# Layer 0's experts: slot comparisons and return matrices written entry by entry, behind the gathered rows

## The chip, the core and the metric

The kernel runs on one core of one Trainium2 chip. The metric is the device time of one execution in microseconds (us), as the median of several runs. The core has a matrix engine (PE, with its weight loads shown apart as PEld), a vector engine (DVE), an activation engine (ACT), a general engine (POOL) and a queue engine for transfers (SP). Each engine works through its own list of instructions in order; an instruction whose input is late holds back all that stand behind it on that engine.

## The reference

The whole program is a decoder of two layers over x of 8 entries, 256 tokens and 256 features: self attention, cross attention and a feed-forward part, twice. The change lies in the feed-forward part of layer 0. There each of 8 experts chooses the 32 tokens (256 / 8) for which it has the largest gates, works on their normed rows, scales the results by the gate values and writes them back to their tokens. The write is a "set": where several experts chose one token, the last of them counts.

```python
def _L0_ffn_ref(x, gate_w, experts):
    B, N, D = x.shape
    E = gate_w.shape[-1]
    M = N // E
    gate_logits = jnp.einsum('bnd,de->bne', x, gate_w)
    competitive_gates = sinkhorn(gate_logits)
    vals, idx = jax.lax.top_k(jnp.swapaxes(competitive_gates, -1, -2), M)
    gate_values = jnp.swapaxes(vals, -1, -2)
    routed_indices = jnp.swapaxes(idx, -1, -2)
    b_idx = jnp.arange(B)[:, None, None]
    routed = x[b_idx, routed_indices]
    routed = jnp.transpose(routed, (2, 0, 1, 3))
    outputs = jnp.einsum('ebmd,edf->ebmf', routed, experts)
    outputs = outputs * jnp.transpose(gate_values, (2, 0, 1))[..., None]
    vals_bmed = jnp.transpose(outputs, (1, 2, 0, 3))
    routed_back = jnp.zeros_like(x).at[b_idx, routed_indices].set(vals_bmed)
    return routed_back

x = x + _L0_ffn_ref(_layernorm(x, axis=-1), L0_ffn_gate_w, L0_ffn_experts)
```

## The kernel before

All of x stays on the chip. The attention parts are a list of 24 units: for each pair of entries two self attentions and two cross attentions of layer 0, then eight self attentions of layer 1. A loop goes through the units. The core of a unit has eight pieces: score products `st` (L334), exponentials `pT` (L343), value products `o` (L366), and after the second group of heads a copy of `o` to `oT` on DVE (L387). Behind each piece the loop emits a piece of the neighbouring units (the end of the one before, the preparation of the one after), and then one step of the experts, `next(experts_at)`. The experts are written as a generator, `chosen_experts(b0, nb)`, that works on a group of two entries (nb = 2) and pauses at each `yield`. There are four groups. So the sequence of the program interleaves three streams.

The order of the program is not yet the order on the engines. A planner in the build step places each instruction by its position in the program, as a rank, and by when it takes its inputs to be there; it may set a later instruction ahead of an earlier one on the same engine. The order that came out can be read in the trace.

The preparation of a self attention unit runs, for each of two halves of the tokens, the products `qk` and `v` (L274), the rotation `qc` and `qs` on DVE (L413, L429), in layer 0 an addition to `qc` on POOL (L464), and the sum `qkr` (L465), on POOL for the first half and on DVE for the second. Then PE transposes `qkr` twice: `tr` (L283), which is copied to `kT`, and `qps` (L474), which becomes `qm` (L312, L310).

In a group of the experts:

- the gates are formed and balanced, and the 32 best tokens of each of 8 experts and 2 entries are found on DVE (L671 to L675). That gives 256 slots per entry. Their token numbers and gate values go to memory and come back in two layouts: `idx_row` (the 256 token numbers of an entry along the free side, in all partitions) and `by_half`;
- six steps pass, then PE turns `by_half` into `cps` (L689) and DVE copies it to `col` (L691): for each half of the slots of an entry, the token number and gate value of each slot, one per partition;
- **slot comparisons** (L696): for each entry and half one operation on DVE compares the token numbers of all slots (`idx_row`) with that of the slot in the partition (`col`), multiplies by `later` (1 where the other slot comes later) and sums into a column of `over`. A slot with `over` zero is the last for its token. Two small operations (L706, L707) make `weight` from this: the gate value where `over` is zero, else 0. They work on the four columns of the group at once;
- per entry: two **gathering matrices** `pick` (L714) and two **matrices of the return** `put` (L715), 128x256 each, made on POOL by comparing with a constant row; a `yield`; PE forms the gathered rows `rps` (L274), ACT copies them to `rT` (L722); a `yield`; PE multiplies by the experts, `y` (L728), DVE scales by `weight` into `ys` (L738); a `yield`; PE multiplies by `put`, `back` (L274), and DVE adds that to x (L745).

In the program a group's step with `col` and the comparisons comes after `values(0)` and the first half's `qk` of a unit; the first entry's `pick` and `put` after the next scores; its `rps` after `values(1)`, the copy to `oT` and the second half's `qk` and rotation. The second entry's steps follow behind the first entry's `back`; its `rps` falls in the next unit. Each small tile (`put`, `pick`, `junk`, `weight` and others) has two buffers.

Of the kernel before, what the change touches and what calls it, by code (L numbers as in the profile page):

```python
# [28 lines left out]
F32 = mybir.dt.float32  # L29
# [4 lines left out]
ALU = mybir.AluOpType  # L34
# [4 lines left out]
P = 128  # L39
B, S, D = 8, 256, 256  # L40
# [115 lines left out]
def plain(  # L156
# [4 lines left out]
    nc = tc.nc  # L161
# [83 lines left out]
    def norm_stats(views, eps, pool, tag):  # L245

        n = len(views)
        st = pool.tile([P, 2, 6], F32, tag=f"{tag}st", name=f"{tag}st")
        mv = pool.tile([P, 2, 2], F32, tag=f"{tag}mv", name=f"{tag}mv")
        for i, v in enumerate(views):  # L250
            nc.vector.bn_stats(st[:, i, :], v)
            nc.vector.bn_aggr(mv[:, i, :], st[:, i, :])
        ve = pool.tile([P, 2], F32, tag=f"{tag}ve", name=f"{tag}ve")
        nc.vector.tensor_scalar(ve[:, :n], mv[:, :n, 1], eps, None, ALU.add)  # L254
        rs = pool.tile([P, 2], F32, tag=f"{tag}rs", name=f"{tag}rs")
        nc.gpsimd.tensor_tensor(rs[:, :n], ve[:, :n], mhalf[:, :n], ALU.pow)  # L256
        return mv, rs

    def normed(dst, src, mv, rs, i):
        return nc.vector.tensor_scalar(dst, src, mv[:, i, 0:1], rs[:, i : i + 1], ALU.subtract, ALU.mult)  # L260
# [332 lines left out]
    bwork = w_exp.enter_context(tc.tile_pool(name="b2", bufs=2, side="right"))  # L593
    experts = one.tile([P, E, 2, D], F32, name="experts")
    later = one.tile([P, 2, S], F32, name="later")
    num = one.tile([P, S], F32, name="num")
# [32 lines left out]
    def chosen_experts(b0, nb):  # L629

        xn = bwork.tile([P, 2 * nb, D], F32, tag="xnb", name="xnb")
        g = bwork.tile([P, nb, 2, E], F32, tag="g", name="g")
        for b in range(nb):
            mv, rs = norm_stats([x[:, 2 * (b0 + b) + t, :] for t in range(2)], 1e-5, small, "ln")
            for t in range(2):
                normed(xn[:, 2 * b + t, :], x[:, 2 * (b0 + b) + t, :], mv, rs, t)
            xnT = transposed(xn[:, 2 * b : 2 * b + 2, :], work, mm, "xnT")
            yield
            lg = mm.tile([P, 2, D], F32, tag="mm", name="lg")
            for t in range(2):  # L640
                for c in range(2):
                    product(lg[:, t, :E], xnT[:, c, bass.ts(t, P)], gate[:, c, :], c == 0, c == 1)
            nc.vector.tensor_scalar(g[:, b], lg[:, :, :E], 1e-6, None, ALU.max)
            yield

        gt = bwork.tile([P, 2, nb, E], F32, tag="gt", name="gt")
        for it in range(8):
            cs = mm.tile([P, nb, E], F32, tag="mm", name="cs")
            for t in range(2):
                product(cs, ones, g[:, :, t, :], t == 0, t == 1)  # L650
            rc = bwork.tile([P, nb, E], F32, tag="rc", name="rc")
            nc.vector.reciprocal(rc, cs)
            nc.vector.tensor_tensor(g, g, rc.unsqueeze(2).to_broadcast([P, nb, 2, E]), ALU.mult)
            rsum = bwork.tile([P, nb, 2], F32, tag="rsum", name="rsum")
            nc.vector.tensor_reduce(rsum, g, AX.X, ALU.add)
            rr = bwork.tile([P, nb, 2], F32, tag="rr", name="rr")
            nc.vector.reciprocal(rr, rsum)
            dst = gt.rearrange("p t b e -> p b t e") if it == 7 else g
            nc.vector.tensor_tensor(dst, g, rr.unsqueeze(3).to_broadcast([P, nb, 2, E]), ALU.mult)
            yield  # L660


        vps = mm.tile([nb * E, S], F32, tag="mm", name="vps")
        for t in range(2):
            nc.tensor.transpose(vps[:, bass.ts(t, P)], gt[:, t].rearrange("p b e -> p (b e)"), ident)
        v = bwork.tile([nb * E, S], F32, tag="v", name="v")
        nc.scalar.copy(v, vps)
        top = bwork.tile([nb * E, 2, TOP], F32, tag="top", name="top")
        place = bwork.tile([nb * E, TOP], U32, tag="place", name="place")
        for r in range(0, TOP, 8):  # L670
            nc.vector.max(top[:, 1, r : r + 8], v)  # L671
            nc.vector.max_index(place[:, r : r + 8], top[:, 1, r : r + 8], v)
            if r + 8 < TOP:
                nc.vector.match_replace(v, top[:, 1, r : r + 8], v, NEG)
        nc.vector.tensor_copy(top[:, 0, :], place)  # L675

        slots = dram.tile([2, nb * S], F32, name=f"slots{b0}")
        nc.sync.dma_start(slots.rearrange("k (q r) -> q k r", r=TOP), top)
        idx_row = bwork.tile([P, nb, S], F32, tag="idx_row", name="idx_row")
        nc.sync.dma_start(  # L680
            idx_row.rearrange("p b s -> p (b s)"), slots[0:1, :].to_broadcast([P, nb * S])
        )
        by_half = bwork.tile([2 * nb, 2, P], F32, tag="by_half", name="by_half")
        nc.sync.dma_start(by_half, slots.rearrange("k (q s) -> q k s", s=P))
        for _ in range(6):
            yield
        cps = mm.tile([P, 2, 2 * nb], F32, tag="mm", name="cps")
        for k in range(2):
            nc.tensor.transpose(cps[:, k, :], by_half[:, k, :], ident[: 2 * nb, : 2 * nb])  # L689
        col = bwork.tile([P, 2, 2 * nb], F32, tag="col", name="col")  # L690
        nc.vector.tensor_copy(col, cps)  # L691
        over = bwork.tile([P, 2 * nb], F32, tag="over", name="over")
        for q in range(2 * nb):
            b, h = q // 2, q % 2
            junk = bwork.tile([P, S], F32, tag="junk", name="junk")
            nc.vector.scalar_tensor_tensor(  # L696
                junk,
                idx_row[:, b, :],
                col[:, 0, q : q + 1],
                later[:, h, :],  # L700
                ALU.is_equal,
                ALU.mult,
                accum_out=over[:, q : q + 1],
            )
        weight = bwork.tile([P, 2 * nb], F32, tag="weight", name="weight")
        nc.vector.tensor_scalar(weight, over, 0.0, None, ALU.is_equal)  # L706
        nc.vector.tensor_tensor(weight, weight, col[:, 1, :], ALU.mult)  # L707
        yield

        for b in range(nb):  # L710
            pick = bwork.tile([P, 2, S], F32, tag="pick", name="pick")
            put = bwork.tile([P, 2, S], F32, tag="put", name="put")
            for t in range(2):
                nc.gpsimd.tensor_scalar(pick[:, t, :], idx_row[:, b, :], tokid[:, t : t + 1], None, ALU.is_equal)  # L714
                nc.gpsimd.tensor_scalar(put[:, t, :], num, col[:, 0, 2 * b + t : 2 * b + t + 1], None, ALU.is_equal)  # L715
            yield
            rps = mm.tile([P, 2, S], F32, tag="mm", name="rps")
            for c in range(2):
                for t in range(2):
                    product(rps[:, c, :], xn[:, 2 * b + t, bass.ts(c, P)], pick[:, t, :], t == 0, t == 1)  # L720
            rT = bwork.tile([P, 2, S], F32, tag="rT", name="rT")
            nc.scalar.copy(rT, rps)  # L722
            yield
            y = mm.tile([P, 2, D], F32, tag="mm", name="y")
            for e in range(E):
                rows = slice(TOP * (e % 4), TOP * (e % 4) + TOP)
                for c in range(2):
                    nc.tensor.matmul(  # L728
                        y[rows, e // 4, :],
                        rT[:, c, TOP * e : TOP * (e + 1)],  # L730
                        experts[:, e, c, :],
                        start=c == 0,
                        stop=c == 1,
                    )
            ys = bwork.tile([P, 2, D], F32, tag="ys", name="ys")
            for h in range(2):
                q = 2 * b + h
                nc.vector.tensor_scalar(ys[:, h, :], y[:, h, :], weight[:, q : q + 1], None, ALU.mult)  # L738
            yield
            back = mm.tile([P, 2, D], F32, tag="mm", name="back")  # L740
            for t in range(2):
                for h in range(2):
                    product(back[:, t, :], put[:, h, bass.ts(t, P)], ys[:, h, :], h == 0, h == 1)
            xb = x[:, 2 * (b0 + b) : 2 * (b0 + b) + 2, :]
            nc.vector.tensor_tensor(xb, xb, back, ALU.add)  # L745
            yield
# [2019 lines left out]
```

## Time and profile before

| what | value |
|---|---|
| runs | 1375.85, 1377.11, 1380.27 us; median 1377.11 |
| profiled execution, its own time | 1368.84 us |
| span of its profile | 1367.0 us |
| mean granted clock of PE | 0.993 |
| slot comparisons L696 | 16, median 0.684 us (0.473 to 1.521) |
| weights L706 and L707 | 4 each, median 0.245 and 0.275 us |
| return matrices L715 | 16, median 0.972 us (0.914 to 1.212) |
| gathering matrices L714 | 16, median 0.921 us |
| the four groups, first comparison at | 194.02, 301.14, 405.88, 506.34 us |

Times in the profile are counted from the start of the span. A line of the time order gives the start, the time busy (over several instructions where it ends in x2 or more), engine, line, operation, what is written and read, and in brackets how long the engine had been idle and what ended that. A window's line gives the busy time of each engine in a stretch, with the number of instructions, and behind them the granted clock of PE (1.00 is full), the share of the transfer engines and GB/s.

### The profile page before, as it was taken

How to read it: one execution, taken by the hardware profiler on the slowest of the kernel's cores; microseconds unless marked ns; L12 is line 12 of the kernel's file. 1: busy time of each engine (PE TensorE's matmuls, PEld its weight loads, DVE VectorE, ACT ScalarE, POOL GpSimd, SP SyncE). 2: the span in 40 equal slices, each digit the busy share in tenths (PEclk: the TensorE clock that was granted, in tenths of full speed). 3: DMA queues.
4: the chain of work that ended last, by engine and by line, in shares of the span. 5: the costliest groups of instructions: out<-in, count | busy, mean ns of one | idle time of the engine just before them, and what ended most of it. 6: DMA issues, size and time to landing. Idle time of an engine off the chain costs nothing.

```text
span 1367.0 us, 30959 instructions
## 1 busy us (share of the span) xinstructions
PE 1328.8 (97%) x13210; PEld 924.9 (68%) x13210; DVE 575.7 (42%) x1632; ACT 482.6 (35%) x778; POOL 384.7 (28%) x481
## 2 busy tenths in 40 slices
PE   6999999999999999999999999999999999999998
PEld 3666756755766766665667676776767657688886
DVE  5343463473465564444224323232432447322234
ACT  2455443543543433531313223231322313022222
POOL 4232051051033242420214243241424421400004
PEclk9999999999999999999999999999999999999999
DMA  8970000000000003200011010101101110779954
GB/s 309 337 234 17 9 25 1 17 19 7 2 9 2 2 9 105 106 1 1 17 48 32 17 33 17 34 16 48 33 17 33 65 32 8 285 314 409 394 224 130
DMA packets 46930, 116.71 MB, mean 85 GB/s; under 512 B 8272, under 2 KB 30400, under 8 KB 42432
## 3 DMA queue, kind: packets, MB, share of 16 engines
q1 hardware_dynamic: 38912, 92.74, 19.9%
q0 software_dynamic: 5152, 18.89, 3.8%
q10 hardware_dynamic: 2720, 3.02, 0.6%
q8 instruction: 106, 1.74, 0.5%
q14 instruction: 40, 0.33, 0.1%
HBM read 104.00 MB, written 27.93 MB: 97 GB/s over the span
## 4 chain that ended last, share of the span: by engine, by line
PE 81%; DVE 5%; POOL 5%; issue 3%; ACT 1%; DMA 1%; SPq 0%; POOLq 0%; ACTq 0%; DVEq 0%
PE st L334 9%; PE o L366 9%; PE h L274 6%; PE v L274 6%; PE k L274 5%; PE wo L274 4%; PE ox L1372 4%; PE stx L1334 4%; PE out L1754 3%; PE out L1563 3%; PE qk L274 3%; PE tr L283 3%; PE q L274 2%; PE den L1348 2%; PE ao L274 2%
## 5 line engine op out<-in xcount | busy, mean ns | idle before, releaser
L366 PE MATMUL o<-pT,padv 128*64 128x256 f32 (+1 forms) x1536 | 172.6, 367 | 0.9 <-POOL pT L346 0.9
L343 ACT ACTIVATE pT<-st 128x1024 f32<-128x1024 f32 (+1 forms) x128 | 110.6, 915 | 87.6 <-PE st L334 86.4
L366 PEld LDWEIGHTS o<-pT,padv 128*64 128x64 f32 x1536 | 103.6, 138 | 53.7 <-issue 11.6
L334 PE MATMUL st<-qm,kT 64*128 64x256 f32 (+1 forms) x1024 | 116.9, 366 | 0.7 <-DVE qm L312 0.6
L334 PEld LDWEIGHTS st<-qm,kT 64*128 64x128 f32 x1024 | 89.6, 188 | 26.1 <-issue 15.8
L1340 POOL TENSOR_TENSOR both<-pTx 128x512 f32<-128x512 f32 x64 | 82.0, 1305 | 46.0 <-ACT pTx L1338 38.9
L274 PE MATMUL h<-xrT,w 128*64 128x128 f32 (+1 forms) x1936 | 87.0, 250 | 1.1 <-issue 1.1
L274 PEld LDWEIGHTS h<-xrT,w 128*64 128x64 f32 x1936 | 84.4, 137 | 4.0 <-issue 1.7
L343 ACT ACTIVATE pT<-st,kbias 128x1024 f32<-128x1024 f32 x64 | 67.9, 1112 | 28.8 <-PE st L334 28.7
L1338 ACT ACTIVATE pTx<-stx 128x1024 f32<-128x1024 f32 x64 | 62.2, 1022 | 42.3 <-PE stx L1334 40.3
L256 POOL TENSOR_TENSOR lnrs<-lnve,mhalf 128x2 f32<-128x2 f32 x48 | 33.7, 705 | 147.1 <-DVE lnve L254 95.2
L949 DVE TENSOR_TENSOR midr<-sl,h 128x128 f32<-128x128 f32 x102 | 29.3, 288 | 95.3 <-PE h L274 65.3
L334 PE MATMUL st<-qm,memk 64*128 64x256 f32 x512 | 68.8, 393 | 0.4
L1334 PE MATMUL stx<-qTx,kTx 64*128 64x256 f32 x512 | 64.3, 391 | 2.5 <-ACT pTx L1338 2.5
L274 PE MATMUL qk<-l_wqkv,xnT 128*64 128x512 f32 x256 | 62.6, 610 | 0.7 <-ACT xnT L286 0.7
L346 POOL TENSOR_SCALAR_AFFINE_SELECT pT<-pT 128x512 f32<-128x512 f32 x64 | 40.0, 645 | 82.0 <-ACT pT L343 78.7
L1372 PE MATMUL ox<-pTx,vx 128*64 128x256 f32 x512 | 61.1, 381 | 0.0
L948 ACT ACTIVATE sl<-h 128x128 f32<-128x128 f32 (+1 forms) x108 | 31.8, 294 | 79.7 <-PE h L274 55.8
L1334 PEld LDWEIGHTS stx<-qTx,kTx 64*128 64x128 f32 x512 | 46.1, 186 | 20.3 <-ACT pTx L1338 7.2
L274 PE MATMUL wo<-wout_x,oT 128*64 128x256 f32 x512 | 58.0, 379 | 0.0
L334 PEld LDWEIGHTS st<-qm,memk 64*128 64x128 f32 x512 | 48.0, 186 | 14.8 <-issue 4.7
L1423 POOL TENSOR_TENSOR oT<-oT,rs 128x512 f32<-128x512 f32 x30 | 37.3, 1276 | 64.2 <-DMA rs<-rd 64.2
(393 smaller groups left out, 2302.8 us busy)
## 6 DMA issues: line engine op xcount, KB each, us to landing
w<-packs SPq DMA_DIRECT2D x22, 1408.0 KB
w<-packs SPq DMA_DIRECT2D x22, 768.0 KB
rs<-rd SPq DMA_DIRECT2D x16, 512.0 KB
packs<-L_ffn_w_eDF SPq DMA_DIRECT2D x8, 704.0 KB
packs<-L_ffn_w_eDF SPq DMA_DIRECT2D x8, 640.0 KB
packs<-L_ffn_w_eFD SPq DMA_DIRECT2D x8, 640.0 KB
ctxT<-ctx_T SPq DMA_DIRECT2D x8, 512.0 KB
wkv_x<-L_xattn_Wkv POOLq DMA_DIRECT2D x1, 4096.0 KB, 15.8
```

Of the source, the lines that this page charges most:

```text
L274: nc.tensor.matmul(out[h], lhsT[:, h], rhs, start=start, stop=stop, skip_group_check=True)
L283: nc.tensor.transpose(ps[:, c, t * P : (t + 1) * P], rows[:, t, c * P : (c + 1) * P], ident)
L334: nc.tensor.matmul(st[:, g, i, :n], kT[rows, c, bass.ts(kt, P)], qm[rows, 2 * mq + i, c, q0:], start=True, stop=True,)
L343: nc.scalar.activation(pT[:, :, :, :n], st[:, :, :, :n], AF.Exp, scale=scale, **kb)
L346: nc.gpsimd.affine_select(out=pT[:, :, :, :P], in_=pT[:, :, :, :P], compare_op=ALU.is_ge, fill=0.0, base=0, pattern=[[0, 2], [0, 2], [1, P ...
L366: nc.tensor.matmul(o[64 * i : 64 * i + 64, mq, q0:], v_pad[:, kt, 4 * c + 2 * mq + i, 2 * g : 2 * g + 2, :], pTs[kt][:, g, i, : S - q0], s ...
L1334: nc.tensor.matmul(st[:, g, kt, :], kT[rows, c, bass.ts(kt, P)], qT[rows, c, :], start=True, stop=True)
L1338: nc.scalar.activation(pT, st, AF.Exp, scale=scale)
L1340: nc.gpsimd.tensor_tensor(both, pT[:, :, 0, :], pT[:, :, 1, :], ALU.add)
L1372: nc.tensor.matmul(o[XD * g : XD * (g + 1), i, :], v[:, kt, 2 * (c2 + i) + g, :], pT[:, g, kt, :], start=kt == 0, stop=kt == 1, skip_group ...
L1563: nc.tensor.matmul(ps, mid[:, i, lo : lo + P], w2[:, i, :], start=i == 0, stop=i == NFC - 1)
L1754: nc.tensor.matmul(ps[h], mid[:, i, h], sets[k % len(sets)][1][:, i, :], start=i == 0, stop=i == NFC - 1, skip_group_check=True,)
```

## The change

The comparisons, until now made for both entries of the group right behind `col`, and the `put` matrices, made beside `pick`, are written per entry behind the copy of the gathered rows to `rT`. There `put` and the comparison of each half follow each other, and then the two weight operations for the entry's two columns. So there are eight weight operations of each kind instead of four, each half as wide; comparisons and matrices keep their number and shape. The `yield` that stood behind the comparisons stays, so the number of steps is the same.

```diff
         over = bwork.tile([P, 2 * nb], F32, tag="over", name="over")
-        for q in range(2 * nb):
-            b, h = q // 2, q % 2
-            junk = bwork.tile([P, S], F32, tag="junk", name="junk")
-            nc.vector.scalar_tensor_tensor(
-                junk,
-                idx_row[:, b, :],
-                col[:, 0, q : q + 1],
-                later[:, h, :],
-                ALU.is_equal,
-                ALU.mult,
-                accum_out=over[:, q : q + 1],
-            )
         weight = bwork.tile([P, 2 * nb], F32, tag="weight", name="weight")
-        nc.vector.tensor_scalar(weight, over, 0.0, None, ALU.is_equal)
-        nc.vector.tensor_tensor(weight, weight, col[:, 1, :], ALU.mult)
         yield
 
         for b in range(nb):
...
             for t in range(2):
                 nc.gpsimd.tensor_scalar(pick[:, t, :], idx_row[:, b, :], tokid[:, t : t + 1], None, ALU.is_equal)
-                nc.gpsimd.tensor_scalar(put[:, t, :], num, col[:, 0, 2 * b + t : 2 * b + t + 1], None, ALU.is_equal)
             yield
...
             rT = bwork.tile([P, 2, S], F32, tag="rT", name="rT")
             nc.scalar.copy(rT, rps)
+            for h in range(2):
+                q = 2 * b + h
+                nc.gpsimd.tensor_scalar(put[:, h, :], num, col[:, 0, q : q + 1], None, ALU.is_equal)
+                junk = bwork.tile([P, S], F32, tag="junk", name="junk")
+                nc.vector.scalar_tensor_tensor(
+                    junk,
+                    idx_row[:, b, :],
+                    col[:, 0, q : q + 1],
+                    later[:, h, :],
+                    ALU.is_equal,
+                    ALU.mult,
+                    accum_out=over[:, q : q + 1],
+                )
+            of_b = slice(2 * b, 2 * b + 2)
+            nc.vector.tensor_scalar(weight[:, of_b], over[:, of_b], 0.0, None, ALU.is_equal)
+            nc.vector.tensor_tensor(weight[:, of_b], weight[:, of_b], col[:, 1, of_b], ALU.mult)
             yield
             y = mm.tile([P, 2, D], F32, tag="mm", name="y")
```

## The prediction

> **What bounds the kernel now.** I read the page first, then the matrix engine's list of waits, then the order of time on POOL, DVE and PE around each of the four runs of the experts, and at last the granted clock in short windows there.
>
> ```profile
> span 1367.0 us, 30959 instructions
> PE 1328.8 (97%) x13210; PEld 924.9 (68%) x13210; DVE 575.7 (42%) x1632; ACT 482.6 (35%) x778; POOL 384.7 (28%) x481
> ```
>
> PE is busy for all but 38 us. An edit on DVE and POOL can only pay where PE waits for them. The matrix engine's waits, in us in total, times and longest:
>
> ```profile
> PE tr L283 <- DVE qkr L465: 9.4, 6, 2.7
> ...
> PE back L274 <- DVE ys L738: 0.6, 1, 0.6
> ```
>
> Between 180 and 560 us the first of these is 6.8 us in four waits. The time order shows three of them right behind the touched lines, one per group of two entries: 2.68 us at 199.2, 2.50 us at 306.5, 0.51 us at 411.8. (The fourth, 1.10 us at 493.7, lies before the comparisons of its group.) POOL in group 1 (start, us):
>
> ```profile
> 187.55 3.65 POOL L714 TENSOR_SCALAR pick<-idx_row,tokid 128x256 f32<-128x256 f32 x4 [2.70 <-DMA idx_row<-slots]
> 191.17 0.71 POOL L256 TENSOR_TENSOR lnrs<-lnve,mhalf 128x2 f32<-128x2 f32 x1
> ...
> 194.69 1.33 POOL L465 TENSOR_TENSOR qkr<-qc,qs 128x512 f32<-128x512 f32 x1
> 196.00 3.91 POOL L715 TENSOR_SCALAR put<-num,col 128x256 f32<-128x256 f32 x4
> 199.88 1.25 POOL L464 TENSOR_TENSOR qc<-qc,turned 128x512 f32<-128x512 f32 x1
> ```
>
> DVE beside it:
>
> ```profile
> 191.92 0.73 DVE L260 TENSOR_SCALAR xnb<-x,lnmv,lnrs 128x256 f32<-128x256 f32 x2 [6.19 <-POOL lnrs L256]
> ...
> 193.83 0.15 DVE L691 COPY col<-cps 128x8 f32<-128x8 f32 x1
> ...
> 197.37 0.32 DVE L706 TENSOR_SCALAR weight<-over 128x4 f32<-128x4 f32 x1
> 197.72 0.16 DVE L707 TENSOR_TENSOR weight<-weight,col 128x4 f32<-128x4 f32 x1
> 197.80 0.68 DVE L387 COPY oT<-o 128x512 f32<-128x512 f32 x1
> 198.40 0.68 DVE L413 TENSOR_TENSOR qc<-qk,cos 128x512 f32<-128x512 f32 x1
> ...
> 201.17 0.69 DVE L465 TENSOR_TENSOR qkr<-qc,qs 128x512 f32<-128x512 f32 x1 [1.42 <-POOL qc L464]
> ```
>
> From 194.02 to 197.33 DVE makes the four comparisons (L696). The four matrices of the return stand on POOL ahead of the second half's `qc`; that ends at 201.13, `qkr` at 201.86, and only then can PE transpose it:
>
> ```profile
> 201.91 0.69 PE L283 MATMUL tr<-ident,qkr 128*128 128x128 f32 x2 [2.68 <-DVE qkr L465]
> ```
>
> The wait also costs clock. Windows (length, PE, PEld, DVE, ACT, POOL, clock):
>
> ```profile
> 203.40:207.00 3.60, 3.60 (x35) 1.49 (x34) 1.50 (x2) 1.37 (x2) 0.00 (x0) 0.50 0.00 0
> 309.90:312.90 3.00, 3.00 (x34) 1.40 (x34) 1.50 (x2) 1.54 (x3) 0.00 (x0) 0.60 0.00 0
> 412.30:415.00 2.70, 2.68 (x38) 1.73 (x38) 1.02 (x2) 1.76 (x3) 0.00 (x0) 1.00 0.03 6
> ```
>
> After the waits of 2.68 and 2.50 us the granted clock is 0.50 and 0.60, after 0.51 us it stays 1.00. The same matmuls, from the second transposes to the start of the next `st`, take 10.92 us in group 1 (201.91 to 212.83), 9.66 in group 2 (309.02 to 318.68) and 8.03 in group 3 (412.32 to 420.35): clock lost, 2.89 and 1.63 us.
>
> **Does a later place in the program become a later place on the engine?** This decides the case, and the trace lets it be read. The second entry's matrices are written in the program after `back` of the first entry, far behind the `qc` of L464; yet POOL ran all four ahead of it. `xnb` at 191.92 belongs to the next group, which the program begins two units later, and it stands ahead of this unit's `col`. So the planner gives an idle engine whatever is ready. Both moved operations are ready once `col` is there, before and after. What could go ahead of them now that they rank lower? On DVE, the copy of `oT` and the `qc` and `qs` of the second half; on POOL, its `qc`. Their inputs come from PE, whose order follows `cps` with 2.00 us of `st`, 1.95 of `o` and 1.89 of `qk`: some 4 us from `cps` to `oT`, some 5.8 to `qk`. In the planner's view, without the late slot list that holds up POOL here (2.70 us) and through `lnrs` DVE (6.19 us), the comparisons (3.31 us with the collisions they have here) end before `oT` is ready, and the matrices (3.91) before `qc`. I take it that the order stays.
>
> **The parts.**
> - Comparisons, 16, and matrices, 16: the same operations, written later, nothing removed: 0. Neither issues a DMA; no transfer of SP's or POOL's queue is passed.
> - Weights: 8 small operations become 16, half as wide. One pair holds DVE from the start of its first to the next copy: 197.37 to 197.80, 304.47 to 304.91, 409.08 to 409.60, so 0.43, 0.44, 0.52 us. The half-wide form isn't in the trace. A 128x2 addition (L254) takes 0.17, against 0.17 to 0.32 here, so halving the width saves nothing to speak of: I take the pair as it is, with 0.30 below (two of 0.15, the shortest 128x2) and 0.71 above (0.32 and 0.39, the longest of each). Behind it in DVE's queue: `oT`, `qc`, `qs`, `qkr`.
> - Group 1 and 2: the added pair is hidden behind the matrices on POOL. DVE's `qc` ends at 199.08 and 306.19; POOL is free at 199.91 and 307.02: cover 0.83 each, over 0.44. 0; without that cover 0.87 for both.
> - Group 3 (layer 1, no addition on POOL): `qkr` follows directly on DVE, and PE already waits: +0.52. If the second entry's pair falls behind `oT` and `qkr`, with some comparisons, up to the wait of 0.51 is gained instead.
> - Group 4: after `oT` (509.57) DVE idles 1.09 us for `qk`, which hides the pair: 0; without that cover 0.6.
> - A finer wait: `ys` of the first entry now needs only its own pair, but the weights were ready at 197.9 for a `ys` at 207.15: 0.
>
> Sum: 1368.84 (span 1367.0 and 1.84 around it) + 0.52 = 1369.36. The median of the runs lies 8.27 above the profiled execution: **1377.6 us**.
>
> [...] The windows show the clock at half after waits of 2.68 and 2.50 us. [...]
>
> [...]
>
> **The rivals.**
> - *Faster: the work does move behind the second half's rotation, on both engines.* In group 1 DVE goes from `col` (193.98) to `oT` and `qc`; POOL takes `qc` at 196.02, ends at 197.3; `qkr` is there at 198.0, before PE wants it at 199.2. The three waits go, 5.69 us, and the lost clock, 4.52: 1377.1 - 10.2 = **1366.9**. For it: this is exactly the work in front of `qc`, and the sum of comparisons and pairs comes near the 4 us that DVE has. Against: the second entry's matrices, which already ranked below `qc`, went before it. One engine alone doesn't do it: with POOL free but DVE as it is, `qc` comes at 199.1 instead of 199.88, and a wait of 1.9 stays.
> - *Slower: the comparisons land between `y` and `ys`.* A comparison pair and its weights, placed behind DVE's `qm`, hold `ys`, and `back` waits. From `ys`'s end to `back` there are 1.25 (208.03 to 209.28), 1.26, 0.53 and 1.44 us in the four groups. The collided pair of group 1 (194.02 to 196.31) and its weights are 2.29 + 0.43 = 2.72: late by 1.47 + 1.46 + 2.19 + 1.28 = 6.4, so **1383.5**. It passes 4.1 us once some 2.15 us stand in front of `ys`. For it: `ys` is the next reader, and the new place is just ahead of it. Against: DVE has idle time in between (1.42, 1.63 and 0.76 us in group 1). If waits reach 2.5 us the clock falls and each costs 1.6 to 2.9 more.
> - *Nothing moves* is the forecast itself. Its own range: -0.5 (group 3) to +3.6 (0.71, and the clock lost for 2.89 after a wait that is then 1.22); with the lowest run 1.26 under the median, **1375.3 to 1380.7**.
>
> **Chances.** A measurement of this kernel tells some 0.3%, 4.1 us, from no change. The order stays, 0.45: all of it within. Work moves and the waits go, 0.28: faster. `ys` or a neighbour is held, 0.27: slower. Range 1366 to 1384: all of the first, most of the second (its full gain is 1366.9, a partial one lies above), half of the third; about 0.8.
>
> **What would show it.** If I am right, POOL again has four matrices in a row ahead of `qc`, DVE has `col`, four comparisons and four small operations ahead of or around `oT`, PE waits 2.7, 2.5 and about 1.0 us for `qkr`, and the clock is 0.5 to 0.6 behind the first two. If `qc` stands ahead of the matrices and these two waits are missing, the planner did follow the program, and the step on the order is wrong. If a wait of `back` for `ys` of over 1 us appears, it is the slower rival. The same order with another time would make my pricing of the pair wrong.

## The result

Twelve runs of the changed kernel have a median of 1378.74 us (1377.33 to 1382.05), twelve of the kernel before 1379.02 (1375.85 to 1380.50). The ratio, estimated over all these runs and so not quite the quotient of the two medians (0.9998), is 1.0002, 95% interval 0.9993 to 1.0011, which is -1.0 to +1.5 us: no change that a measurement can tell. Forecast were 1377.6 us, in a range of 1375.3 to 1380.7 if the order stays, and a difference within the 0.3% that a measurement can tell from none.

The page of the profile after opens with:

```profile
span 1376.4 us, 30967 instructions
...
PE 1328.0 (96%) x13210; PEld 925.4 (67%) x13210; DVE 575.9 (42%) x1640; ACT 482.1 (35%) x778; POOL 384.0 (28%) x481
```

Eight instructions more, all on DVE (1640 against 1632): the halved weight operations. Compared instruction by instruction, PE, ACT, POOL and SP carry the same list in the same order as before (two matmuls near the end of the program are recorded the other way round, as they also are between the two profiles of the kernel before). DVE's list differs only where comparisons and weights follow each other. POOL in group 1 (start, us):

```profile
186.66 3.65 POOL L700 TENSOR_SCALAR pick<-idx_row,tokid 128x256 f32<-128x256 f32 x4 [2.62 <-DMA idx_row<-slots]
190.28 0.71 POOL L256 TENSOR_TENSOR lnrs<-lnve,mhalf 128x2 f32<-128x2 f32 x1
...
193.80 1.34 POOL L465 TENSOR_TENSOR qkr<-qc,qs 128x512 f32<-128x512 f32 x1
195.12 3.98 POOL L710 TENSOR_SCALAR put<-num,col 128x256 f32<-128x256 f32 x4
199.07 1.26 POOL L464 TENSOR_TENSOR qc<-qc,turned 128x512 f32<-128x512 f32 x1
```

All four `put`, now written as L710 behind the gathered rows, still stand in one piece ahead of the second half's `qc`. DVE beside it:

```profile
191.03 0.74 DVE L260 TENSOR_SCALAR xnb<-x,lnmv,lnrs 128x256 f32<-128x256 f32 x2 [6.10 <-POOL lnrs L256]
...
193.13 0.87 DVE L712 SCALAR_TENSOR_TENSOR junk<-idx_row,col,later 128x256 f32<-128x256 f32 x1
...
193.93 1.49 DVE L712 SCALAR_TENSOR_TENSOR junk<-idx_row,col,later 128x256 f32<-128x256 f32 x1
...
195.97 0.28 DVE L722 TENSOR_SCALAR weight<-over 128x2 f32<-128x2 f32 x1
196.04 0.47 DVE L712 SCALAR_TENSOR_TENSOR junk<-idx_row,col,later 128x256 f32<-128x256 f32 x1
196.44 0.08 DVE L712 DVE_READ_ACCUMULATOR junk<-idx_row,col,later 128x1 f32 x1
196.44 0.15 DVE L723 TENSOR_TENSOR weight<-weight,col 128x2 f32<-128x2 f32 x1
196.56 0.32 DVE L722 TENSOR_SCALAR weight<-over 128x2 f32<-128x2 f32 x1
196.91 0.16 DVE L723 TENSOR_TENSOR weight<-weight,col 128x2 f32<-128x2 f32 x1
196.99 0.68 DVE L387 COPY oT<-o 128x512 f32<-128x512 f32 x1
...
200.37 0.69 DVE L465 TENSOR_TENSOR qkr<-qc,qs 128x512 f32<-128x512 f32 x1 [1.43 <-POOL qc L464]
```

The first entry's pair of weights lies around the fourth comparison: it runs while that one does. From the first comparison to `oT` there are 3.86 us (193.13 to 196.99) where there were 3.78. PE's time order for groups 1 and 2 shows the waits that stayed:

```profile
201.11 0.44 PE L283 MATMUL tr<-ident,qkr 128*128 128x128 f32 x2 [2.69 <-DVE qkr L465]
...
201.92 1.97 PE L729 MATMUL y<-experts,rT 128*32 128x256 f32 x32
...
305.49 0.69 PE L283 MATMUL tr<-ident,qkr 128*128 128x128 f32 x2 [2.65 <-DVE qkr L465]
...
306.97 2.82 PE L729 MATMUL y<-experts,rT 128*32 128x256 f32 x32
```

2.69 and 2.65 us against 2.68 and 2.50; group 3 has 0.47 against 0.51. Behind two equal waits the same 32 matmuls `y` take 1.97 and 2.82 us. The windows over them (length, PE, PEld, DVE, ACT, POOL, clock) give the reason:

```profile
201.90:203.90 2.00, 2.00 (x35) 1.17 (x36) 1.12 (x2) 0.96 (x2) 0.00 (x0) 1.00 0.00 0
306.90:309.70 2.80, 2.80 (x33) 1.30 (x32) 1.50 (x2) 1.02 (x2) 0.00 (x0) 0.66 0.00 0
```

The clock stayed full behind the first wait (1.00) and fell behind the second (0.66); the last section shows where.

The span is 9.4 us longer than that of before (1367.0), which is not the change. One wait near the end of the program makes it: PE, then ACT in the same stretch.

```profile
1355.52 1.22 PE L998 MATMUL h<-sums,sums 128*128 128x256 f32 x2 [9.57 <-ACT beside L1022]
```

```profile
1352.28 0.60 ACT L1032 ACTIVATE beside<-h 128x512 f32<-128x512 f32 x1 [5.26 <-remote]
1355.10 0.37 ACT L1022 COPY beside<-h 128x256 f32<-128x256 f32 x1 [2.22 <-remote]
```

The first profile of before has no such wait; its execution of 1368.84 us lay below every timed run of that kernel (1375.85 at the lowest). The second profile of before, below, has it with 9.69 us, and all other profiles taken later have one of 5.3 to 9.7 us at this place. So the 8.27 us between the profiled execution and the median, which the prediction carried along as a difference, is about the size of this wait. What ends it is not seen in the records ("remote"), and no run here tried to find it.

### The profile page after: what moved, and what is told of

It is laid out like the page before. It is cut to its first block, busy times and chain, and to the rows that moved or that the text cites. A ratio compares the mean times of both kernels' runs of the same rounds, so it can differ in the third digit from the quotient of the medians.

```text
span 1376.4 us, 30967 instructions
## 1 busy us (share of the span) xinstructions
PE 1328.0 (96%) x13210; PEld 925.4 (67%) x13210; DVE 575.9 (42%) x1640; ACT 482.1 (35%) x778; POOL 384.0 (28%) x481
## 4 chain that ended last, share of the span: by engine, by line
PE 81%; DMA 6%; DVE 5%; POOL 4%; issue 1%; ACT 1%; SPq 1%; another core or an unknown queue 1%; ACTq 0%; POOLq 0%; DVEq 0%
PE st L334 8%; PE o L366 8%; PE v L274 7%; PE h L274 6%; PE k L274 5%; PE wo L274 5%; PE ox L1373 4%; PE stx L1335 4%; PE out L1755 3%; PE out L1564 3%; PE qk L274 3%; PE q L274 2%; PE tr L283 2%; DMA packs<-L_ffn_w_eDF 2%; PE den L1349 2%; PE ao L274 2%
```

## The experiments

Five kernels tell the theories apart, two more look at what decides the order, and one is the kernel before again. In them `tc.issue_after(x)` makes what is written inside it stand behind instruction `x` on the engine, whatever the planner would choose.

| kernel | median us (runs) | ratio to before | 95% interval |
|---|---|---|---|
| both engines held back | 1370.94 (6) | 0.9939 | 0.9924 to 0.9955 |
| POOL alone held back | 1375.04 (11) | 0.9970 | 0.9959 to 0.9981 |
| DVE alone held back | 1379.54 (12) | 0.9997 | 0.9988 to 1.0005 |
| next group's norms later | 1371.78 (6) | 0.9943 | 0.9925 to 0.9961 |
| norms later, and POOL held back | 1370.65 (6) | 0.9936 | 0.9916 to 0.9955 |
| comparisons held between `qm` and `ys` | 1380.12 (12) | 1.0002 | 0.9992 to 1.0012 |
| written just before `ys`, nothing held | 1378.07 (1) | | |
| before, once more | 1380.48 (1) | | |

The kernel before ran beside them at 1379.47 (16 runs; the first, second, fourth and fifth) and 1379.69 (23 runs; the others).

### Both engines held back

```diff
+                    late["pool"] = nc.gpsimd.tensor_tensor(qc, qc, self.bias[0][:, t, :], ALU.add)
...
+                if t:
+                    late["dve"] = summed
...
+                with tc.issue_after(late["pool"].ins):
                     nc.gpsimd.tensor_scalar(put[:, h, :], num, col[:, 0, q : q + 1], None, ALU.is_equal)
+                with tc.issue_after(late["dve"].ins):
                     nc.vector.scalar_tensor_tensor(
```

> The changed kernel, with an edge that makes the move real: each matrix of the return issues behind the second half's qc on POOL, each comparison behind the second half's qkr on DVE. Theory (in the change only the place in the program moved, the order on the engines did not; the work ahead of qc is what PE waits for): the waits of PE for qkr of 2.7, 2.65 and 0.5 us disappear, 5.8 us, and with them up to 4.5 us of lost clock. But the comparisons (3.3 to 4 us) now stand between qkr and qm, and ys comes behind qm: back has 0.5 us of slack, so I expect back to wait 1 to 1.5 us for ys in three groups. Net -1.5 to -7 us against before (ratio 0.995 to 0.999). The faster rival of the prediction, as it was priced: -10.2 us (0.9926). The rival that the order doesn't matter at all: 1.000, waits for qkr unchanged.

By the ratio the time falls by 8.4 us (interval 6.2 to 10.5). PE, DVE and POOL in group 1:

```profile
198.89 0.66 PE L283 MATMUL tr<-ident,qkr 128*128 128x128 f32 x4
```

```profile
196.93 0.96 DVE L467 TENSOR_TENSOR qkr<-qc,qs 128x512 f32<-128x512 f32 x1 [1.09 <-POOL qc L466]
197.82 0.72 DVE L718 SCALAR_TENSOR_TENSOR junk<-idx_row,col,later 128x256 f32<-128x256 f32 x1
...
202.69 0.87 DVE L745 TENSOR_SCALAR ys<-y,weight 128x256 f32<-128x256 f32 x2
```

```profile
195.63 1.27 POOL L466 TENSOR_TENSOR qc<-qc,turned 128x512 f32<-128x512 f32 x1
196.88 3.96 POOL L715 TENSOR_SCALAR put<-num,col 128x256 f32<-128x256 f32 x4
```

The four transposes run in one piece: the wait is gone, in groups 2 and 3 as well. Nothing takes its place: the waits of `back` for `ys` of 1 to 1.5 us that were expected do not appear. The comparisons fit between `qkr` and `qm`, `ys` comes early enough, and `back` waits 0.6 us once in the whole program, as before. From the first `cps` to the last `back` of group 4 this profile takes 339.7 us (188.6 to 528.3), the two of the kernel before 350.1 and 349.3: the gain arises in this stretch and not at the end of the program. So the work that the change writes later is what PE waits for, and an engine order that really is later pays.

### POOL alone, DVE alone

The same edit with only the first, or only the second, of the two blocks.

> The changed kernel with the edge on POOL alone: matrices behind the second half's qc, comparisons where the planner puts them. Theory: qc on POOL then waits for DVE, whose qc ends 0.8 us before POOL takes it now, so the two waits in layer 0 go from 2.7 to about 1.9 us and group 3 keeps 0.5: -1.6 us. If a wait of 1.9 us no longer brings the clock down, up to 4 us more: ratio 0.9955 to 0.999. Rival (POOL's matrices are the whole cause): both waits disappear, -5.2 us and the clock.

> The changed kernel with the edge on DVE alone: comparisons behind the second half's qkr, matrices where the planner puts them, ahead of qc on POOL. Theory: qc on POOL is still behind the four matrices; PE waits some 2.5 us for qkr in groups 1 and 2 (qc can start a little earlier, as POOL's qkr and the matrices no longer run beside comparisons), none in group 3; then comparisons stand between qkr and qm, and back waits 0.5 to 1.5 us for ys. Net -0.5 to +3, ratio 0.9995 to 1.002. Rival (the comparisons on DVE alone are the cause): the two waits disappear, ratio 0.9945 to 0.996.

POOL alone gives -4.1 us (interval -5.7 to -2.6), DVE alone nothing that can be told (-1.7 to +0.7). PE and POOL with POOL alone held back:

```profile
199.71 0.44 PE L283 MATMUL tr<-ident,qkr 128*128 128x128 f32 x2 [1.59 <-DVE qkr L467]
```

```profile
197.66 1.27 POOL L466 TENSOR_TENSOR qc<-qc,turned 128x512 f32<-128x512 f32 x1 [2.85 <-DVE qc L413]
```

POOL is now free 2.85 us too early, and what is left of the wait (1.59, 1.30 and 0.67 us) is DVE's share: comparisons and weights in front of `oT` and `qc`. The clock stayed full behind both longer waits (`y` 1.97 us each time; a granted clock of 1.00 over 186 to 216 and 290 to 320 us, where before had 0.89 and 0.94). With DVE alone held back the other side is seen:

```profile
200.37 0.69 DVE L467 TENSOR_TENSOR qkr<-qc,qs 128x512 f32<-128x512 f32 x1 [5.00 <-POOL qc L466]
```

DVE waits 5.00 us for POOL, and PE still waits 2.28 and 2.29 us. Both engines hold up the same product, POOL a little longer, and the later of the two counts.

### The next group's norms later

This kernel leaves the change out. It is the kernel before, with the norms of the next group placed behind the `ys` of this group's first entry on DVE.

```diff
         for b in range(nb):
-            mv, rs = norm_stats([x[:, 2 * (b0 + b) + t, :] for t in range(2)], 1e-5, small, "ln")
-            for t in range(2):
-                normed(xn[:, 2 * b + t, :], x[:, 2 * (b0 + b) + t, :], mv, rs, t)
+            with ExitStack() as behind:
+                if "hold" in late:
+                    behind.enter_context(tc.issue_after(late["hold"].ins))
+                mv, rs = norm_stats([x[:, 2 * (b0 + b) + t, :] for t in range(2)], 1e-5, small, "ln")
+                for t in range(2):
+                    normed(xn[:, 2 * b + t, :], x[:, 2 * (b0 + b) + t, :], mv, rs, t)
...
+                scaled = nc.vector.tensor_scalar(ys[:, h, :], y[:, h, :], weight[:, q : q + 1], None, ALU.mult)
+            if b == 0:
+                hold = scaled
...
+        late["hold"] = hold
```

> The kernel before, with one edge: the norms of the next group of experts issue on DVE behind ys of this group's first entry, so their lnrs no longer stands behind pick on POOL and xnb no longer holds DVE for 6 us. Comparisons and matrices stay as they are. Theory (the waits for qkr come from xnb, which waits behind a slot list that lands late): col is there some 4 us earlier, the comparisons run in DVE's idle time, and qkr waits only for POOL: from 2.68, 2.50 and 0.51 us to about 0.5, 0.5 and 0; -4.7 us and up to 4.5 of clock, ratio 0.993 to 0.9966. Rival (comparisons and matrices ahead of qc are the cause wherever they stand): waits stay above 2 us, ratio 0.999 to 1.001.

The time falls by 7.9 us (interval 5.4 to 10.3), with comparisons and `put` where they always were. DVE in group 1:

```profile
188.81 0.16 DVE L698 COPY col<-cps 128x8 f32<-128x8 f32 x1
189.00 0.48 DVE L703 SCALAR_TENSOR_TENSOR junk<-idx_row,col,later 128x256 f32<-128x256 f32 x1
...
190.96 1.12 DVE L713 TENSOR_SCALAR weight<-over 128x4 f32<-128x4 f32 x1
...
192.42 0.69 DVE L387 COPY oT<-o 128x512 f32<-128x512 f32 x1 [0.15 <-PE o L366]
```

POOL beside it:

```profile
193.39 3.61 POOL L722 TENSOR_SCALAR put<-num,col 128x256 f32<-128x256 f32 x4
196.96 1.27 POOL L466 TENSOR_TENSOR qc<-qc,turned 128x512 f32<-128x512 f32 x1
```

In the kernel before, `xnb` of the next group stands ahead of `col`, and waits 6.19 us for `lnrs`; that stands on POOL behind `pick`, which waits for the late slot list. Without it `col` is there at 188.81 and not 193.83. Comparisons and weights end at 192.27, 0.15 us before `oT` can start, so they cost nothing. The waits of the first three groups become 0.3, 0.27 and 0 (the first from the four transposes, 0.92 us against 0.66). So the comparisons are not in the wrong place. They are in the right place and held up by something else. The matrices still hold up `qc` on POOL here: they end at 197.00, and DVE's `qc` is there at 194.83.

### Norms later, and POOL held back

The edit above, together with the change and the block around `put`.

> The changed kernel with both edges that should help: norms of the next group behind ys, matrices of the return behind the second half's qc on POOL; comparisons in DVE's idle time. Theory: all three waits for qkr gone, back doesn't wait: -5.8 us and up to 4.5 of clock, ratio 0.9926 to 0.9958, the fastest of the four. Rival: new waits take their place, ratio above 0.997.

1370.65 us is the lowest median, but its interval holds the ratios of both engines held back (0.9939) and of the norms alone (0.9943): the remedies overlap and don't add. The remaining 0.3 and 0.27 us go. In exchange two weight operations take 1.22 and 1.24 us, at a place where DVE has time.

### Comparisons held between `qm` and `ys`

This builds the slower rival. The block is written directly before `ys`, and the comparisons stand behind DVE's second `qm`.

```diff
+                late["qm"] = nc.vector.tensor_scalar(qm[:, m], ps, masks[:, m : m + 1], None, ALU.mult)
...
+                with tc.issue_after(late["qm"].ins):
                     nc.vector.scalar_tensor_tensor(
...
             ys = bwork.tile([P, 2, D], F32, tag="ys", name="ys")
```

> The changed kernel, with comparisons and matrices written directly before ys, and an edge that holds each comparison behind DVE's second qm, so that they stand between y and ys: the slower rival of the prediction, made on purpose. Matrices stay ahead of qc on POOL (nothing holds them). Theory: POOL still holds qc, so PE waits 2.7 us twice for qkr, group 3 gains its 0.5; three comparisons (0.47 to 0.69 each without a two-tensor operation on POOL beside them) and one to two weight pairs, about 2.2 us, stand ahead of ys, whose slack before back is 0.5: back waits 1.4 to 1.8 us in each of the first three groups. Net +3.5 to +5 us against before, ratio 1.0025 to 1.0036; with a wait of back that brings the clock down, up to 1.008. As priced in the prediction: +6.4 (1.0046). Rival (ys isn't late, DVE has room there): ratio 1.000 or below.

No slower: -1.1 to +1.7 us. PE in group 3 of this kernel:

```profile
410.06 1.97 PE L715 MATMUL y<-experts,rT 128*32 128x256 f32 x32
411.96 2.80 PE L366 MATMUL o<-pT,padv 128*64 128x256 f32 x22
414.93 1.95 PE L274 MATMUL back<-ys,put 128*64 128x256 f32 x16 [0.16 <-DVE ys L742]
416.68 1.49 PE L366 MATMUL o<-pT,padv 128*64 128x256 f32 x10
```

In the changed kernel the pieces are 16 `o`, 16 `back`, 16 `o`. Here they are 22, 16 and 10: PE got six more `o` in front of `back`, and waits 0.16 us. PE's order moved with the later `ys`, which the rival's price of 6.4 us left out by holding that order fixed. The price was also too high for the block itself: it took 2.72 us in front of `ys`, and here, in group 1, four comparisons and the weights that `ys` needs take 1.96 (204.41 to 206.37), while POOL is idle (200.26 to 214.21); each comparison takes 0.47 or 0.48 us. The waits for `qkr` (2.33, 2.25 and 0 us) stay where POOL causes them.

### Written just before `ys`, nothing held

The change with its block one step further back, behind the products `y`, and no edge.

> The changed kernel with comparisons, matrices and weights written one step later still, directly before ys, without any edge. Theory (the place in the program doesn't matter while the engine is idle and the inputs are there): the same order on DVE and POOL, PE waits of about 2.7, 2.6 and 0.5 us for qkr, time as the changed kernel within 0.3%. Rival: something moves, the waits change by over 0.5 us. This profile is also one more look at the clock behind the two long waits: if it always falls after a wait of 2.5 us, it is 0.5 to 0.7 behind both; if it depends on more than the length, it stays 1.00 behind one or both.

PE, DVE, POOL and SP carry the same order, instruction for instruction, as with the change (but for the same two matmuls near the end). The waits are 2.66, 2.68 and 0.57 us. So a second later place in the program did not become a later place on the engine either.

### The kernel before, once more

> The kernel before, for a second profile. Waits of about 2.7, 2.5 and 0.5 us as in the first. On the clock: 0.5 to 0.6 behind both long waits if the length of the wait decides; 1.00 behind one or both if it doesn't alone. On the end of the span: if the profiled execution of before was short by chance (8 us under its median, without the wait of 9.6 us that the changed kernel's profile has some 30 us before its end), this one shows such a wait and a span of about 1376; if the changed program brings that wait, it isn't there.

One run, 1380.48 us, with waits of 2.60, 2.68 and 0.57 us, and `y` slower behind the first two (3.11 and 2.92 us, 1.97 behind the third). It has the wait near the end that its first profile lacked:

```profile
1358.54 1.22 PE L997 MATMUL h<-sums,sums 128*128 128x256 f32 x2 [9.69 <-ACT beside L1021]
```

## Why the prediction was right, point by point

- **The order stays: right.** POOL's order is the same, and DVE's differs only by where a pair of weights stands between comparisons. The further kernel written later still shows the same. The reason given, that in the planner's view this work is finished before `oT` and `qc` can start, fits the run with the norms later: with the delay gone, the comparisons and weights end 0.15 us before `oT` on the chip. For the matrices no run shows it: there they end 2.17 us after the `qc` of DVE that POOL's next operation takes, with `pick` still 2.30 us late for the slot list. What the planner reckons with was not read itself, so its view remains an inference.
- **The added pair, +0.52 us in group 3: mis-sized.** This term of the sum was too large. The prediction took the second pair as a block behind four comparisons. DVE instead got the first pair around the fourth comparison, where its operations ran under it: `weight` L722 is busy 0.28 us from 195.97 while the comparison starts at 196.04. From first comparison to `oT`: 3.72 us before (405.88 to 409.60) and 3.73 after (402.19 to 405.92) in group 3, so +0.01; +0.08 in group 1. The half-wide form did not get cheaper (0.15 to 0.39 us), as assumed; it got hidden. Group 3's wait was therefore 0.47 us, where about 1.0 had been named as a sign. Half a microsecond is below what the times can tell.
- **Waits of groups 1 and 2: right** in size, 2.69 and 2.65 us against the predicted 2.7 and 2.5.
- **Clock behind them: half right.** It fell in group 2 (0.66 over `y`) and not in group 1 (1.00). Such a wait is no certain cost: `y` was slower behind nine of twelve, as the last section shows.
- **The faster rival's mechanism holds, by force.** It did not happen by the change, but with both engines held the three waits go, as it said. It priced 5.69 us of waits and 4.52 of clock, 10.2 together; measured are 8.4, interval 6.2 to 10.5. The waits alone, 5.69, lie under the interval, which fits some clock coming back too (`y` takes 1.97 us in all three groups); how much of the 4.52 is not settled, as the clock does not fall after every such wait.
- **"One engine alone doesn't do it": right for DVE, too strict for POOL.** A wait of 1.9 us was to stay with POOL free; 1.59 stayed, because the comparisons and weights in front of `oT` got shorter once `put` no longer ran beside them (the third 0.48 for 0.68 us, the last weight pair 0.28 from start to `oT` for 0.43). The clock also stayed full (1.00 in both stretches above), and the whole was worth 4.1 us.
- **The slower rival:** its place was built and its price did not appear, since PE's order moved with it and the block took 1.96 us, not 2.72.
- **The sum** was made against the profile's own time, with 8.27 us added for the median. That offset came out about right (the median lies 9.4 above the sum of 1369.36) and hid that a wait of this size was missing from the profile that every other view was read from. It lies far from the changed lines, so it did no harm here. That 1377.6 came so close to 1378.74 is in part luck: it starts from the median of three runs of the kernel before, 1377.11, and twelve gave 1379.02. What held is the forecast of no change.

## What to carry to other kernels

Under a planner, a later place in the program need not move work that is ready early; here two later places moved next to nothing. Compare the order of each engine first; if it is the same, the same time is the first guess. When an engine is late with work that is well placed, look at what stands ahead of that work and what it waits for; here one list arriving late held DVE up by some 5 us, and setting the stalled norms back was worth about as much as forcing the late work behind. Moving work off one engine pays only down to the next engine that holds the same product (here, with POOL freed, 1.59 us of a wait of 2.69 stayed).

## What the runs showed of the hardware

**The clock after a short wait.** Twelve waits of PE between 2.25 and 2.69 us, in six profiles (two of the kernel before, the change, the one written later still, and the two with DVE's comparisons held back), were followed by a slower `y` nine times (2.8 us and more) and by a full-speed one three times (1.97 us, after 2.69, 2.66 and 2.28 us). Behind the shorter waits ahead of `y` (1.59, 1.30 and less) `y` took 1.97 us. So in this band length alone does not decide.

The first profile of before and that of the change show where the clock fell. In each of the two it changes only at edges that lie whole multiples of 3.41 us apart: in that of before it falls at 201.26 us, rises at 208.09, falls at 310.49 and rises at 313.90; in that of the change it falls at 305.38 and rises at 308.79. Windows cut at such edges, from the changed kernel (length, PE, PEld, DVE, ACT, POOL, clock):

```profile
199.57:202.98 3.41, 1.87 (x26) 1.39 (x30) 1.44 (x2) 0.75 (x2) 0.76 (x1) 1.00 0.19 65
202.98:206.39 3.41, 3.41 (x43) 2.11 (x34) 1.53 (x3) 1.21 (x2) 0.00 (x0) 1.00 0.00 0
301.97:305.38 3.41, 0.88 (x8) 0.31 (x4) 1.98 (x5) 1.87 (x2) 2.74 (x3) 1.00 0.27 77
305.38:308.79 3.41, 3.30 (x26) 2.09 (x30) 1.02 (x3) 1.27 (x2) 0.00 (x0) 0.50 0.00 0
308.79:312.20 3.41, 3.41 (x44) 2.04 (x41) 1.42 (x3) 0.69 (x1) 0.00 (x0) 1.00 0.00 0
```

The border at 199.57 lies 31 such steps ahead of the fall at 305.38 and cuts the wait of 2.69 us; PE is busy for 1.87 us of the window that holds most of it, and the clock stays full (1.00). The wait of 2.65 us lies almost wholly in one window, with 0.88 us busy, and the next window runs at half (0.50). The same windows in the kernel before:

```profile
197.85:201.26 3.41, 1.38 (x12) 0.77 (x8) 1.99 (x6) 2.12 (x2) 3.28 (x4) 1.00 0.26 76
201.26:204.67 3.41, 2.76 (x19) 1.80 (x23) 1.35 (x2) 0.98 (x2) 0.00 (x0) 0.50 0.01 4
307.08:310.49 3.41, 1.47 (x18) 1.12 (x22) 1.24 (x2) 1.03 (x2) 1.16 (x1) 1.00 0.27 77
310.49:313.90 3.41, 3.41 (x30) 1.61 (x24) 1.83 (x4) 1.37 (x2) 0.00 (x0) 0.50 0.00 0
```

In these four cases the clock fell where PE was busy for 0.88 to 1.47 us of the window that holds most of the wait, and stayed full at 1.87 us. What lies between, and whether the other eight cases agree, is not shown. The windows stand elsewhere against the program in the two profiles: one begins 0.65 us ahead of the end of the first wait in that of before (201.26, 201.91) and 1.54 us ahead in that of the change (199.57, 201.11). That it is a matter of chance from run to run whether a wait of this length costs clock is the author's estimate from these cases.

**Small DVE operations held for as long as POOL's.** In the kernel with norms later and POOL held back, DVE and POOL:

```profile
190.65 1.22 DVE L731 TENSOR_TENSOR weight<-weight,col 128x2 f32<-128x2 f32 x1
...
191.98 1.24 DVE L731 TENSOR_TENSOR weight<-weight,col 128x2 f32<-128x2 f32 x1
```

```profile
190.38 1.46 POOL L466 TENSOR_TENSOR qc<-qc,turned 128x512 f32<-128x512 f32 x1
191.92 1.27 POOL L467 TENSOR_TENSOR qkr<-qc,qs 128x512 f32<-128x512 f32 x1
```

Operations of 0.15 us elsewhere end at 191.87 and 193.22, in each case 0.03 us behind the end of POOL's two-tensor operation (191.84 and 193.19). A comparison takes 0.48 us with POOL idle (DVE alone held back), 0.47 to 0.72 beside `put` (both engines held back), and 1.49 beside `qkr` on POOL (the change). In these profiles it made more difference what POOL ran than that it ran.
